# Layer 1 with DMA transposes, its scales taken through DRAM and its output matmuls one place later, a beginning written out by hand, and GpSimd additions placed behind their products in layer 2

## The chip, the core and the metric

The kernel runs on one core of one Trainium2 chip. The metric is device time in microseconds (us), as the median of a few runs. Beside it stands one profiled execution, whose trace gives the start, the length and the waits of the instructions on each engine: PE (TensorE), DVE (VectorE), ACT (ScalarE), POOL (GpSimd) and SP (SyncE, which here only issues DMAs).

## What is computed

Three sublayers, each followed by a residual addition and a layer norm, on x of shape (16, 256, 512), all float32:

```python
x = layernorm(x + attention(x))   # 16 heads of 32; causal softmax; q, k, v and output are "bitlinear":
                                  # weights rounded to -1, 0, 1 by their mean size,
                                  # each token rounded to 8 bits by its largest size
x = layernorm(x + mix(ctx, x))    # 32 heads of 8: kv_ij = ctx_i * ctx_j; long convolution of kv
                                  # along the sequence with a kernel for each head, plus D * kv;
                                  # out_j = sum over i of (that)_ij * x_i
x = layernorm(x + ffn(x))         # rms norm, gamma, 8-bit rounding, one ternary matmul 512 x 512
```

The norms and roundings use the sizes that the reference gives: epsilon 1e-5 in the layer norms, 127 steps for a token's largest value, and the mean absolute value for a weight.

## The kernel before

There are two stages. **Layer 1** (attention) takes one batch at a time, 256 tokens in NT = 2 tiles of 128. **Layer 2** (mixing and the feed-forward part) takes one head of the mixing at a time, 32 heads; the rows of a head are 8 inner places by 16 batches. The result of layer 1 stays in SBUF as `x1t`, already turned for layer 2.

Before layer 1 the five weights are loaded, summed (`part`), scaled (`w_mul`), rounded in two passes (L119 and L120 on DVE or POOL) and stored as bfloat16 (L121, on ACT).

Layer 1 is a pipeline over batches, written out by hand in `step(b)`: PE, ACT, DVE and POOL execute in the order of the calls. The scheduler orders SP's DMAs itself. Within a step four groups g of four heads each follow one another, and stages of other batches are set between their parts:

- `scan(b+1, g)`: scores for the maximum, in the PSUM tile `s` of four banks, of which there is one (L252 the mask, L259 the products); DVE takes the maximum (L264). `weigh(b, g)`: scores again in the same `s` (L292, L299), the exponential on ACT (L304, p), and two causal masks on POOL (L308). So `s` goes from scan to maximum to scores to exponential, and to the next scan.
- `values(b, g)`: p times v (L324), and the sums of p by a matmul with `col` (L331), whose right side is 256 and then 128 columns wide. `save_sums`, `divide_sums`, `divide`: the softmax's division, after a transpose on PE.
- `fetch_x`, `fetch_scales`, `fetch_scaled`, `fetch_rounded`: load of x, the tokens' scales, the scaled x on POOL (L135, xq_t), and its rounding on ACT (L141, xq_i). `turn_in`: the scales become a row along the free axis by a matmul with ones (L202), and the rounded x is turned by eight PE transposes (L148) with copies on ACT. `project_qk` and `project_v` (L220, L232) use it.
- `out_scales`, `out_scaled`, `out_rounded`, `turn_out`, `close`: the same for the attention's output (oq_t on DVE, oq_i on ACT, eight PE transposes), and the output matmuls (L387) with the residual on DVE. `moments`, `normalize`, `keep`: the layer norm and the transposed copy into `x1t`.

The rounded tiles of input and output come from one pool of SBUF and share one tag:

```python
def rounded(pool, tag, t):
    xi = pool.tile([P, E], BF16, name=f"{tag}_i", tag="q_i")   # pool ap, bufs=2
    nc.scalar.activation(xi, t, AF.Copy, bias=-MAGIC)
    return xi
```

Layer 2 is ordered by hand in the same way. For a head h, `block(h, lb)` makes the products of the quarter lb: 2(lb+1) matmuls (L546) into y, of which there are two, and on DVE `own` (L553, L556) and `turn` (L563); POOL adds turn to own (L567) directly behind. `read(h, lb)` sums six tiles into `tok` by PE transposes (L574): five of own, and q itself. `second_moments` and `second_norm` (DVE and ACT) end in fq_t (L135) and its rounding fq_i (L141); `turn(h)` transposes that on PE (L148), `feed_forward(h)` multiplies it (L641) and `finish(h)` writes the head out. POOL makes the next head's kv in `multiply` (L521); ACT copies its q.

Of the kernel before, what the change touches and what calls it, by code (L numbers as in the profile page):

```python
# [15 lines left out]
P = 128  # L16
# [16 lines left out]
def decoder_kernel(ctx: ExitStack, tc: tile.TileContext, x, ctx_t, w_q, w_k, w_v, w_o, ker, d_skip, gamma, w_f, out):  # L33
# [5 lines left out]
    first = const.tile([P, S // P, E], F32, name="first")  # L39
# [4 lines left out]
    wl_scope = ExitStack()  # L44
    wl = wl_scope.enter_context(tc.tile_pool(name="wload", bufs=1))
    wp = wl_scope.enter_context(tc.tile_pool(name="wpsum", bufs=1, space=PSUM))


    nc.sync.dma_start(first, x[0].rearrange("(t p) e -> p t e", p=P))
    raw = [wl.tile([P, NB, E], F32, name=f"raw{i}") for i in range(5)]  # L50
    for i, w in enumerate((w_q, w_k, w_v, w_o, w_f)):
        (nc.scalar, nc.sync)[i % 2].dma_start(raw[i], w.rearrange("(c p) o -> p c o", p=P))
    rows = wl.tile([XH, E + P], F32, name="rows")
    nc.scalar.dma_start(rows, ker)
    dsk = wl.tile([XH, 1], F32, name="dsk")
# [12 lines left out]
    mask_f = wl.tile([P, 2, P], F32, name="mask_f")  # L68
# [7 lines left out]
    nc.vector.tensor_copy(mask, mask_f)  # L76


    pick_f = wl.tile([P, NB], F32, name="pick_f")
# [8 lines left out]
    nc.vector.tensor_copy(pick, view(pick_f, 0, [[1, NB], [0, P]]))  # L88
# [10 lines left out]
    for i in range(5):  # L99
        t = raw[i].rearrange("p c o -> p (c o)")  # L100
        early = i < 3
        part = wl.tile([P, 1], F32, name=f"part{i}")
        if early:
            nc.vector.tensor_reduce(part, t, AX.X, ALU.add, apply_absolute_value=True)
        else:
            size = wl.tile([P, NB * E], BF16, name="size")
            nc.scalar.activation(size, t, AF.Abs, accum_out=part)
        total = wp.tile([P, 1], F32, name=f"total{i}", tag=f"total{i % 2}")
        nc.tensor.matmul(total, ones, part, start=True, stop=True)
        mean = wl.tile([P, 1], F32, name=f"mean{i}")  # L110
        nc.vector.tensor_scalar(mean, total, 1.0 / (E * E), 1e-5, ALU.mult, ALU.max if i < 4 else ALU.add)
        w_mul = wl.tile([P, 1], F32, name=f"w_mul{i}")
        nc.vector.reciprocal(w_mul, mean)
        nc.vector.reciprocal(w_inv[:, i : i + 1], w_mul)
        if i == 0:
            nc.vector.tensor_scalar(q_scale, w_inv[:, 0:1], 1.0 / math.sqrt(DH), None, ALU.mult)

        engine = nc.vector if i in (0, 2) else nc.gpsimd
        engine.tensor_scalar(t, t, w_mul, MAGIC, ALU.mult, ALU.add)  # L119
        engine.tensor_scalar(t, t, MAGIC + 1.0, MAGIC - 1.0, ALU.min, ALU.max)  # L120
        nc.scalar.activation(weights[i].rearrange("p c o -> p (c o)"), t, AF.Copy, bias=-MAGIC)  # L121
    wq, wk, wv, wo, wf = weights

    nc.vector.tensor_tensor(rows[:, P - 1 : P], rows[:, P - 1 : P], dsk, ALU.add)
    nc.sync.dma_start(taps, rows)
    wl_scope.close()


    kept = ctx.enter_context(tc.tile_pool(name="kept", bufs=1))
    x1t = kept.tile([P, XH, NB, XD, B], F32, name="x1t")  # L130
# [29 lines left out]
    with ExitStack() as l1:  # L160
        xp = l1.enter_context(tc.tile_pool(name="xp", bufs=2))
        ap = l1.enter_context(tc.tile_pool(name="ap", bufs=2))
        sp = l1.enter_context(tc.tile_pool(name="sp", bufs=3))
        hp = l1.enter_context(tc.tile_pool(name="hp", bufs=3))
        qk = l1.enter_context(tc.tile_pool(name="qk", bufs=3))
# [11 lines left out]
        def fetch_x(m, b):  # L177
            if b == 0:
                m.x = first
            else:  # L180
                m.x = xp.tile([P, NT, E], F32, name="xt")
                nc.sync.dma_start(m.x, x[b].rearrange("(t p) e -> p t e", p=P))

        def fetch_scales(m):
            amax = sp.tile([P, NT], F32, name="amax")
            nc.vector.tensor_reduce(amax, m.x, AX.X, ALU.max, apply_absolute_value=True)
            m.mul, m.inv = absmax_scales(sp, "x", amax, NT)
            m.v_mul = sp.tile([P, NT], F32, name="v_mul")
            nc.vector.tensor_scalar(m.v_mul, m.inv, w_inv[:, 2:3], None, ALU.mult)

        def fetch_scaled(m):
            m.xt = [scaled(ap, f"xq{t}", m.x[:, t, :], m.mul[:, t : t + 1], nc.gpsimd) for t in range(NT)]
            m.diag = kp.tile([P, NT, P], F32, name="diag")
            for t in range(NT):
                nc.gpsimd.tensor_scalar(m.diag[:, t, :], ident, m.inv[:, t : t + 1], None, ALU.mult)
# [4 lines left out]
        def turn_in(m):  # L200
            row = ps.tile([P, S], F32, name="row", tag="misc")
            nc.tensor.matmul(row, ones, m.diag.rearrange("p t k -> p (t k)"), start=True, stop=True)  # L202
# [5 lines left out]
            m.p = {}  # L208
            m.qt = qk.tile([P, NB, S], F32, name="qt")
            m.kt = qk.tile([P, NB, S], F32, name="kt")  # L210
            m.va = qk.tile([P, NT, NH, DH], F32, name="va")

        def project_qk(m, i):
            dst, w, scale = ((m.qt, wq, q_scale), (m.kt, wk, w_inv[:, 1:2]))[i % 2]
# [14 lines left out]
        def project_v(m, t):  # L229
            acc = ps.tile([P, NH, DH], F32, name="acc_v", tag="misc")  # L230
# [55 lines left out]
        def weigh(m, g):  # L286
# [25 lines left out]
            m.p[g] = p  # L312

        def values(m, g):
# [13 lines left out]
            for j, (q0, src) in enumerate(((0, slice(0, S)), (P, slice(S, S + P)))):  # L328
                for r in range(4):
                    rows = slice(DH * r, DH * (r + 1))  # L330
                    nc.tensor.matmul(  # L331
                        m.sums[rows, q0:S], col[:, g, :], p[:, r, src],
                        start=(g == 0 and j == 0), stop=(g == NB - 1 and j == 1),
# [8 lines left out]
        def save_sums(m):  # L342
            m.st = kp.tile([P, S], F32, name="sums_s")
            nc.vector.tensor_copy(m.st, m.sums)

        def divide_sums(m):
# [6 lines left out]
            m.o = ap.tile([P, NT, E], F32, name="o")  # L353
# [17 lines left out]
        def out_scaled(m):  # L371
            m.ots = [scaled(ap, f"oq{t}", m.o[:, t, :], m.mul_o[:, t : t + 1]) for t in range(NT)]
# [4 lines left out]
        def turn_out(m):  # L377
            m.oit = kp.tile([P, NT, NB, P], BF16, name="oit")
            for t in range(NT):
                transposed(ps, m.oit[:, t], m.oi[t])  # L380

        def close(m):
# [8 lines left out]
            m.st6 = sp.tile([P, NT, 6], F32, name="st")  # L391
            nc.vector.bn_stats(m.st6[:, 0, :], m.r1[:, 0, :])

        def moments(m):
            mv = m.mv = sp.tile([P, NT, 2], F32, name="mv")
            nc.vector.bn_stats(m.st6[:, 1, :], m.r1[:, 1, :])
            for t in range(NT):
                nc.vector.bn_aggr(mv[:, t, :], m.st6[:, t, :])
# [15 lines left out]
        def keep(m, b):  # L414
            nh = P // XD
            for t in range(NT):
                tp = ps.tile([P, NB, P], F32, name="tp1", tag="misc")
                for c in range(NB):
                    nc.tensor.transpose(tp[:, c, :], m.r1[:, t, c * P : (c + 1) * P], ident)
                nc.scalar.copy(  # L420
                    x1t[:, t * nh : (t + 1) * nh, :, :, b].rearrange("p h c i -> p c h i"),
                    tp.rearrange("p c (h i) -> p c h i", i=XD),
                )
# [5 lines left out]
        def step(b):  # L429


            for g in range(NB):
                on(scan, b + 1, g)
                if g == 0:
                    on(fetch_x, b + 3, b + 3)
                    on(fetch_again, b - 1, b - 1)
                    on(turn_in, b + 2)
                    on(moments, b - 2)
                    on(values, b - 1, NB - 1)
                    on(weigh, b, 0)  # L440
                    on(save_sums, b - 1)
                    on(project_qk, b + 2, 0)
                    on(normalize, b - 2)
                    on(divide_sums, b - 1)
                    on(divide, b - 1, 0)
                    on(divide, b - 1, 1)
                elif g == 1:
                    on(project_qk, b + 2, 1)
                    on(out_scales, b - 1)
                    on(values, b, 0)  # L450
                    on(weigh, b, 1)
                    on(project_qk, b + 2, 2)
                    on(keep, b - 2, b - 2)
                elif g == 2:
                    on(out_scaled, b - 1)
                    on(project_v, b + 2, 0)
                    on(values, b, 1)
                    on(weigh, b, 2)
                    on(project_qk, b + 2, 3)
                    on(fetch_scales, b + 3)  # L460
                    on(project_v, b + 2, 1)
                    on(out_rounded, b - 1)
                else:
                    on(turn_out, b - 1)
                    on(lay, b + 1, b + 1)
                    on(fetch_scaled, b + 3)
                    on(values, b, 2)
                    on(weigh, b, 3)
                    on(close, b - 1)
                    on(lay_turned, b + 1, b + 1)  # L470
                    on(fetch_rounded, b + 3)

        by_hand = {mybir.EngineType.PE, mybir.EngineType.Activation, mybir.EngineType.DVE, mybir.EngineType.Pool}
        on(fetch_x, 0, 0)
        on(fetch_scales, 0)
        on(fetch_scaled, 0)
# [266 lines left out]
```

## Time and profile before

| what | value |
|---|---|
| time, median of 3 runs | 1001.84 us (1001.75 to 1002.99) |
| profiled execution | 1000.92 us; span 999.2 us, clock 0.977 |
| PE busy | 886.3 us (89%) |
| DVE busy | 731.0 us (73%) |
| POOL busy | 493.9 us (49%) |
| ACT busy | 415.7 us (42%) |
| first scan of layer 1 starts | 45.8 us |
| step 0 / step 1 / step 13 of layer 1 start (copy `low`) | 61.9 / 87.7 / 416.6 us |
| first product of layer 2 starts | 514.3 us |

Shares are of the span. A busy share is an average over stages with different limits, so it is read by stage. "Idle before, releaser" beside an instruction says how long its engine had stood still and what it waited for last. The last columns of a stretch are the TensorE clock that was granted (1.00 is full), the busy share of the DMA engines, and GB/s. The page's list of DMA issues gives KB for each and the median time from issue to landing.

### The profile page before, as it was taken

What the parts mean: (1) busy time and instruction counts of PE and PEld (TensorE: products, weight loads), DVE (VectorE), ACT (ScalarE), POOL (GpSimd) and SP (SyncE); (2) the same over time, 40 slices, a digit from 0 to 9 for tenths busy, and PEclk for the clock granted to TensorE, in tenths of its full rate; (3) what the DMA queues carried; (4) which work ended last, traced back from release to release, by engine and by line L of the source; (5) the groups of instructions that cost most, each with busy time, mean ns of one, the idle gap of its engine ahead of it and who ended that gap; (6) DMA issues with size and microseconds to landing.
All of it is one profiled execution on the core that took longest, in us unless ns stands there. A gap on an engine that the chain in (4) does not pass through costs nothing.

```text
span 999.2 us, 21479 instructions
## 1 busy us (share of the span) xinstructions
PE 886.3 (89%) x8554; PEld 639.6 (64%) x8554; DVE 731.0 (73%) x1819; ACT 415.7 (42%) x651; POOL 493.9 (49%) x569
## 2 busy tenths in 40 slices
PE   1489999999999999997669999999999999999993
PEld 1356666666666666665437777777777777777772
DVE  6465777777777777766326888888888888888885
ACT  2533566666656656655531322222232223223222
POOL 4412322323223323312238777777777777677761
PEclk9999999999999999999959999999999999999996
DMA  9000111010111110000032122212212221222100
GB/s 318 25 23 23 44 44 44 26 41 23 44 44 44 44 44 23 23 23 23 12 95 53 49 74 64 70 53 74 64 53 70 65 73 49 74 64 63 44 22 22
DMA packets 54739, 53.19 MB, mean 53 GB/s; under 512 B 19120, under 2 KB 35504, under 8 KB 54640
## 3 DMA queue, kind: packets, MB, share of 16 engines
q1 hardware_dynamic: 52816, 48.33, 15.7%
q10 hardware_dynamic: 1824, 3.49, 1.0%
q8 instruction: 68, 1.11, 0.5%
q14 instruction: 31, 0.25, 0.1%
HBM read 43.34 MB, written 8.47 MB: 52 GB/s over the span
## 4 chain that ended last, share of the span: by engine, by line
PE 57%; DVE 28%; ACT 6%; issue 4%; DMA 2%; POOL 2%; SPq 0%; ACTq 0%; DVEq 0%; POOLq 0%
PE y L546 11%; PE acc L220 6%; PE s L292 6%; PE pv L324 5%; PE tok L574 5%; PE s L259 4%; DVE own L553 4%; PE sums L331 4%; DVE turn L563 3%; PE acc_f L641 3%; PE acc_o L387 3%; PE acc_v L232 3%; PE tp L148 3%; DVE full L601 2%; PE s L252 2%
## 5 line engine op out<-in xcount | busy, mean ns | idle before, releaser
L546 PE MATMUL y<-kv,w 128*128 128x288 f32 x1280 | 335.5, 410 | 4.4 <-DMA c<-in_ctx_t 2.9
L546 PEld LDWEIGHTS y<-kv,w 128*128 128x128 f32 x1280 | 235.3, 192 | 60.9 <-POOL kv L521 6.1
L567 POOL TENSOR_TENSOR own<-own,turn 128x512 f32<-128x512 f32 x128 | 162.3, 1268 | 125.1 <-DVE inv_root L597 64.0
L308 POOL TENSOR_SCALAR_AFFINE_SELECT p<-p 128x512 f32<-128x512 f32 x128 | 78.5, 638 | 256.5 <-ACT p L304 256.5
L521 POOL TENSOR_TENSOR kv<-c 128x512 f32<-128x512 f32 (+1 forms) x192 | 186.3, 991 | 3.3 <-DMA w<-taps 3.3
L264 DVE TENSOR_REDUCE nmax<-s 128x4 f32<-128x512 f32 (+1 forms) x128 | 116.7, 954 | 42.3 <-PE s L259 41.1
L553 DVE TENSOR_TENSOR own<-y,q 128x512 f32<-128x512 f32 x128 | 88.2, 689 | 76.8 <-PE y L546 66.6
L304 ACT ACTIVATE p<-s 128x1536 f32<-128x1536 f32 x64 | 93.1, 1454 | 88.4 <-PE s L299 88.4
L574 PE MATMUL tok<-ident,own 128*128 128x128 f32 x640 | 90.7, 273 | 0.0
L590 ACT ACTIVATE root<-quarter 128x2 f32<-128x2 f32 x64 | 13.0, 203 | 163.4 <-DVE quarter L588 163.4
L574 PEld LDWEIGHTS tok<-ident,own 128*128 128x128 f32 x640 | 74.1, 141 | 8.9
L220 PE MATMUL acc<-xit,w 128*128 128x256 bf16 x512 | 67.8, 277 | 5.8 <-ACT xit L149 5.8
L563 DVE TENSOR_TENSOR turn<-y,q 128x384 f32<-128x384 f32 x128 | 70.0, 547 | 0.0
L292 PE MATMUL s<-qt,kt 32*128 32x256 f32 (+1 forms) x1024 | 60.6, 351 | 2.6 <-DVE nmax L264 2.5
L220 PEld LDWEIGHTS <-w 128*128 128x128 bf16 x512 | 46.1, 99 | 23.3 <-issue 13.4
L259 PE MATMUL s<-kt,qt 32*128 32x128 f32 (+1 forms) x1024 | 60.5, 351 | 0.0
L324 PE MATMUL pv<-p,va 128*32 128x256 f32 (+1 forms) x1024 | 55.6, 332 | 4.7 <-POOL p L308 3.3
L292 PEld LDWEIGHTS s<-qt,kt 32*128 32x128 f32 x1024 | 47.1, 186 | 17.1 <-issue 14.8
L649 ACT ACTIVATE res<-r,shift,res 128x512 f32<-128x512 f32 x32 | 26.0, 813 | 71.9 <-DVE shift L605 71.9
L331 PE MATMUL sums<-p,col 128*32 128x256 f32 (+1 forms) x1024 | 54.4, 329 | 0.0
L224 DVE SCALAR_TENSOR_TENSOR qt<-acc,q_scale,inv_row 128x512 f32<-128x512 f32 x32 | 24.0, 750 | 39.5 <-PE acc L220 39.4
L622 ACT ACTIVATE x<-tok,shift,res 128x512 f32<-128x512 f32 x32 | 24.9, 777 | 65.0 <-DVE shift L605 65.0
(126 smaller groups left out, 1391.1 us busy)
## 6 DMA issues: line engine op xcount, KB each, us to landing
xr<-in_x SPq DMA_DIRECT2D x16, 512.0 KB, 3.6
c<-in_ctx_t SPq DMA_DIRECT2D x32, 256.0 KB, 3.4
w<-taps SPq DMA_DIRECT2D x32, 256.0 KB, 4.1
out_y<-res SPq DMA_DIRECT2D x32, 256.0 KB, 2.0
xt<-in_x SPq DMA_DIRECT2D x15, 512.0 KB, 3.6
c<-in_ctx_t SPq DMA_DIRECT2D x32, 128.0 KB, 3.2
raw<-in_w_q ACTq DMA_DIRECT2D x1, 1024.0 KB, 8.8
raw<-in_w_k SPq DMA_DIRECT2D x1, 1024.0 KB, 11.5
```

The source lines that it names most:

```text
L220: nc.tensor.matmul(acc[:, j, :], w[:, c, o * P : (o + 1) * P], m.xit[:, c].rearrange("p t k -> p (t k)"), start=(c == 0), stop=(c == NB - 1),)
L259: nc.tensor.matmul(s[:, r, lo:hi], m.qt[rows, g, q0 : q0 + P], m.kt[rows, g, 0:nk], start=False, stop=True, skip_group_check=True,)
L264: nc.vector.tensor_reduce(view(m.nmax, t * NH + g, [[NB, 4]]), s[:, :, cols], AX.X, ALU.max, negate=True)
L292: nc.tensor.matmul(s[:, r, lo:hi], m.kt[rows, g, k0 : k0 + P], m.qt[rows, g, q0:S], start=(lo == 0), stop=False, skip_group_check=True,)
L324: nc.tensor.matmul(acc[rows, q0:S], m.va[:, j, 4 * g + r, :], p[:, r, src], start=(j == 0), stop=(j == 1), skip_group_check=True, tile_pos ...
L331: nc.tensor.matmul(m.sums[rows, q0:S], col[:, g, :], p[:, r, src], start=(g == 0 and j == 0), stop=(g == NB - 1 and j == 1), skip_group_ch ...
L521: nc.gpsimd.tensor_tensor(kv[:, :, at : at + n * B].rearrange("p c (i b) -> p c i b", b=B), c[:, :, i : i + n, :], c[:, :, i + d : i + d + ...
L546: nc.tensor.matmul(y[:, Y0 + k * HALF : Y0 + (k + 1) * HALF], lhs, kv[:, mb, k * HALF : (k + 1) * HALF], start=(mb == 0), stop=(mb == lb),)
L553: nc.vector.tensor_tensor(own[:, 0:4, :], view(y, Y0 + AT, [[P, 4], [1, P]]), view(q, base, [[B, 4], [1, P]]), ALU.mult)
L563: nc.vector.tensor_tensor(view(t, B, [[P + B, 3], [1, P]]), view(y, Y0 + AT + P, [[P, 3], [1, P]]), view(q, base, [[0, 3], [1, P]]), ALU.mult,
L567: nc.gpsimd.tensor_tensor(own[:, 0:4, :], own[:, 0:4, :], t, ALU.add)
L574: nc.tensor.matmul(tok[:, lb, :], lhsT=part, rhs=ident, is_transpose=True, start=(n == 0), stop=(n == len(parts) - 1),)
```

## The change

**Layer 1.** From batch 2 on, the rounded input and, for every batch, the rounded output are turned by DMA transposes on SP's queue (`turn_in` for batch b+3, `turn_out`), not by PE. The scales are written to DRAM as a line and read back to all partitions (`fetch_line`), where a matmul with ones had made the row. `both`, the sum on POOL of two parts of p, makes the second sums matmul complete, so that the first need only be 128 wide. The output's scaling moves from DVE to POOL, `save_sums` from DVE to ACT. `close` is called for b-2 instead of b-1, in the second group. The order of the whole step is new, and SP's DMAs follow the order of the calls too.

**The beginning.** The weights load into the space of `x1t` (`lent`), and their sums, scales and roundings are single calls placed by hand: w_q and w_k on DVE, w_v's rounding on POOL behind the first scans' inputs, w_o and w_f in steps -1 and 0 (`begin_late`).

**Layer 2.** q's own term is folded into own by (y + 1) x q on DVE, so `read` sums five tiles. `add` (POOL) is called apart from `block` and later. `turn(h-2)` comes after block 0 of the next step, where `turn(h-1)` stood after block 3; `feed_forward` and `finish` move with it.

```diff
-        by_hand = {mybir.EngineType.PE, mybir.EngineType.Activation, mybir.EngineType.DVE, mybir.EngineType.Pool}
+        by_hand = {mybir.EngineType.PE, mybir.EngineType.Activation, mybir.EngineType.DVE, mybir.EngineType.Pool, mybir.EngineType.SP}
...
+        def fetch_line(m):
+            line = lines_pool.tile([NT, P], F32, name="line")
+            nc.sync.dma_start(line.rearrange("t p -> p t"), m.inv)
+            m.inv_row = ap.tile([P, S], F32, name="inv_row")
+            nc.sync.dma_start(m.inv_row, bass.AP(line.tensor, line.offset, [[0, P], [1, S]]))
...
         def turn_in(m):
-            row = ps.tile([P, S], F32, name="row", tag="misc")
-            nc.tensor.matmul(row, ones, m.diag.rearrange("p t k -> p (t k)"), start=True, stop=True)
-            m.inv_row = ap.tile([P, S], F32, name="inv_row")
-            nc.scalar.copy(m.inv_row, row)
             m.xit = ap.tile([P, NB, NT, P], BF16, name="xit")
             for t in range(NT):
-                transposed(ps, m.xit[:, :, t, :], m.xi[t])
+                nc.sync.dma_start_transpose(m.xit[:, :, t, :], m.xi[t])
...
+            both = bp.tile([P, 4, P], F32, name="both")
+            nc.gpsimd.tensor_tensor(both, p[:, :, P : 2 * P], p[:, :, 2 * P : 3 * P], ALU.add)
+            m.p[g], m.both[g] = p, both
...
-            for j, (q0, src) in enumerate(((0, slice(0, S)), (P, slice(S, S + P)))):
+            for q0, src in ((0, p[:, :, 0:P]), (P, m.both[g])):
                 for r in range(4):
                     nc.tensor.matmul(
-                        m.sums[rows, q0:S], col[:, g, :], p[:, r, src],
+                        m.sums[rows, q0 : q0 + P], col[:, g, :], src[:, r, :],
...
-            m.ots = [scaled(ap, f"oq{t}", m.o[:, t, :], m.mul_o[:, t : t + 1]) for t in range(NT)]
+            m.ots = [scaled(ap, f"oq{t}", m.o[:, t, :], m.mul_o[:, t : t + 1], nc.gpsimd) for t in range(NT)]
...
-                transposed(ps, m.oit[:, t], m.oi[t])
+                nc.sync.dma_start_transpose(m.oit[:, t], m.oi[t])
...
+            # the new order of step(b)
+            scan(b+1, 0); fetch_x(b+4); fetch_again(b-1); project_qk(b+2, 0)
+            values(b-1, 3); save_sums(b-1); weigh(b, 0); divide_sums(b-1); divide(b-1, 0 and 1)
+            scan(b+1, 1); project_qk(b+2, 1); values(b, 0); out_scales(b-1); weigh(b, 1)
+            fetch_scaled(b+3); out_scaled(b-1); fetch_rounded(b+3); turn_in(b+3); close(b-2)
+            begin_late(b+4, 0)      # b < 1: sum, scale and first rounding of w_o, w_f
+            scan(b+1, 2); moments(b-2); out_rounded(b-1); turn_out(b-1); project_qk(b+2, 2)
+            values(b, 1); weigh(b, 2); project_qk(b+2, 3); project_v(b+2, 0); normalize(b-2)
+            scan(b+1, 3); project_v(b+2, 1); values(b, 2); weigh(b, 3); keep(b-2, 0 and 1)
+            lay(b+1); lay_turned(b+1); fetch_scales(b+4); fetch_line(b+4); values_scale(b+4)
...
+            nc.vector.scalar_tensor_tensor(
+                own[:, 0, :], view(y, Y0 + AT, [[1, P]]), 1.0, view(q, base, [[1, P]]), ALU.add, ALU.mult
+            )
             nc.vector.tensor_tensor(
-                own[:, 0:4, :], view(y, Y0 + AT, [[P, 4], [1, P]]), view(q, base, [[B, 4], [1, P]]), ALU.mult
+                own[:, 1:4, :], view(y, Y0 + AT + P, [[P, 3], [1, P]]), view(q, base + B, [[B, 3], [1, P]]), ALU.mult
             )
...
-            nc.gpsimd.tensor_tensor(own[:, 0:4, :], own[:, 0:4, :], t, ALU.add)
-            terms.insert(0, view(q, base, [[1, P]]))
...
+                on(multiply, h + 1, 0); on(add, h - 1, 3)
                 on(block, h, 0)
-                on(feed_forward, h - 2)
+                on(turn, h - 2)
                 on(read, h - 1, 2)
-                on(multiply, h + 1, 0)
+                on(multiply, h + 1, 1)
                 on(block, h, 1)
-                on(finish, h - 2, h - 2)
+                on(feed_forward, h - 2); on(add, h, 0)
                 on(read, h - 1, 3)
-                on(multiply, h + 1, 1)
+                on(multiply, h + 1, 2)
                 on(second_moments, h - 1)
                 on(block, h, 2)
                 on(copy, h + 1)
+                on(add, h, 1)
                 on(read, h, 0)
-                on(multiply, h + 1, 2)
+                on(finish, h - 2, h - 2)
                 on(multiply, h + 1, 3)
                 on(second_norm, h - 1)
                 on(block, h, 3)
-                on(turn, h - 1)
+                on(add, h, 2)
                 on(read, h, 1)
```

The step's new order is shown condensed, several calls to a line. The beginning by hand, in the order of its calls: scales, rounding and PE transposes of batch 0; size of w_q (DVE) and w_k (ACT); scale, rounding and store of each; scales of batch 1; size of w_v (ACT); rounding of batch 1; q and k of batch 0; PE transposes of batch 1; scale, rounding (POOL) and store of w_v.

## The prediction

> **What bounds the kernel now.** I read the page's 40 slices first (two stages, a slow seam at slices 19 to 21), then busy time by stretch, then the timeline of one period of each stage. In the first view the columns are start, length, busy time of PE, weight loads, DVE, ACT and POOL (instructions in brackets), then the granted clock.
>
> ```profile
> 180.00:300.00 120.00, 118.05 (x1723) 80.72 (x1720) 87.87 (x172) 73.97 (x103) 33.89 (x54) 1.00 0.11 37
> ...
> 486.00:487.00 1.00, 1.00 (x20) 0.50 (x12) 0.00 (x0) 0.37 (x1) 0.00 (x0) 0.50 0.00 0
> ...
> 700.00:850.00 150.00, 140.13 (x745) 108.29 (x744) 124.56 (x370) 42.29 (x83) 112.44 (x105) 1.00 0.21 62
> ```
>
> Layer 1 is TensorE end to end (118 of 120 us). Layer 2 has PE at 93% and DVE at 83%. The timeline (start, length, engine) gives the periods and two limits behind PE:
>
> ```profile
> 252.28 0.37 ACT L284 COPY low<-tpn 128x256 bf16<-128x256 bf16 x1 [0.41 <-PE tpn L282]
> 279.67 0.37 ACT L284 COPY low<-tpn 128x256 bf16<-128x256 bf16 x1 [0.41 <-PE tpn L282]
> ...
> 450.01 0.60 PE L252 MATMUL s<-mask,ident_h 128*128 128x256 bf16 x4 [0.16 <-ACT p L304]
> 453.51 0.94 PE L292 MATMUL s<-qt,kt 32*128 32x256 f32 x16 [0.60 <-DVE nmax L264]
> 454.71 1.45 ACT L304 ACTIVATE p<-s 128x1536 f32<-128x1536 f32 x1 [2.01 <-PE s L299]
> 456.22 0.60 PE L252 MATMUL s<-mask,ident_h 128*128 128x256 bf16 x4 [0.58 <-ACT p L304]
> ...
> 484.28 0.92 PE L148 MATMUL tp<-ident_h,oq_i 128*128 128x128 bf16 x8 [2.13 <-ACT oq_i L141]
> 487.30 1.67 PE L292 MATMUL s<-qt,kt 32*128 32x256 f32 x16
> ...
> 716.05 0.61 DVE L135 TENSOR_SCALAR fq_t<-xn,mul 128x512 f32<-128x512 f32 x1
> 717.43 0.40 PE L148 MATMUL tp<-ident_h,fq_i 128*128 128x128 bf16 x4 [0.89 <-ACT fq_i L141]
> 720.71 1.76 PEld L546 LDWEIGHTS y<-kv,w 128*128 128x128 f32 x8
> 723.03 0.69 DVE L553 TENSOR_TENSOR own<-y,q 128x512 f32<-128x512 f32 x1 [0.32 <-PE tok L574]
> ```
>
> One step (a batch) takes 27.39. Late in layer 1, where PE has little left, a group of heads still takes 6.21 (450.01 to 456.22): one s buffer goes scan, maximum, scores, exponential, next scan. Four groups make 24.8, so layer 1 can gain at most about 2.6 a step. The clock halved after a PE gap of 2.13, and L292 took 1.67 instead of 0.94. In layer 2 a head takes 14.49, of which PE waits 0.89 for fq_i.
>
> **The change part by part.**
>
> *PE in layer 1.* Removed per step, start to start: row 0.53 (253.48 to 254.01), input transposes 0.72, output transposes 0.85, and sums over 256 instead of 384 columns, 0.64 x 1/3 = 0.21, four times: 2.95. PE would need 24.4. It is no longer the bound.
>
> *The chain that takes over.* In a normal group: scan 1.40, projection 0.97, values 1.20, to the scores 3.57; the scores' weight load to the exponential 1.20; exponential and next scan 1.51: 6.28. Three groups keep that. The second does not. POOL now runs, in order, the masks of the second group, the sum `both`, fetch_scaled, out_scaled; ACT runs exponential 1, xq_i twice, oq_i twice, ot, exponential 2. xq_i and oq_i share a tag with two buffers, so oq_i may be written only when the DMA transposes have read xq_i. ACT therefore waits for a DMA, and ot and exponential 2 are queued behind it, PE's fourth scan behind those. Before, PE had read the same buffers at once. From exponential 1 to exponential 2: 1.45, gap 0.13, masks 1.23, `both` 1.25 (L567, the same POOL addition, 1.27 each), xq_t twice 1.37, hop 0.1, xq_i 0.61, L, oq_i 0.57, ot 0.3 = 7.0 + L. L runs from the end of the second xq_i to the landing of its transpose.
>
> No transpose by DMA is in this trace. From below: the 256 KB store of out_y lands in 2.0 us, L = 2.1. Nearest row: 128 KB of c in 256-byte pieces,
>
> ```profile
> out_y<-res SPq DMA_DIRECT2D x32, 256.0 KB, 2.0
> c<-in_ctx_t SPq DMA_DIRECT2D x32, 128.0 KB, 3.2
> ```
>
> L = 3.3. Against the change speaks the Trainium skill, VectorE: DVE Perf Modes, "The three transpose paths": 1309 ns for 128x128 by DMA. Four blocks are an estimated 5.2, a second transpose queued behind the first brings L to about 10. I take 4.0, nearer the row: that 128 KB take 3.2 where 256 KB in longer pieces take 3.4 says pieces count and not bytes, and a transpose writes more, shorter pieces.
>
> *The clock.* PE's idle before the fourth scan is about L. Gaps of 2.13 (at 484) and 3.02 (at 61.6) were each followed by about 3.2 us at 0.50; one of 1.60 (at 462) was not. TensorE: Matmul & The Clock Gate, Part 1, puts the fall after an idle window of about 3.4 us. By the page only L above 3.4 costs; by the row, which decides, any L above about 2. 3.2 us at half speed delay the last group's scores by 1.6. A step is 3 x 6.28 + 7.0 + 4.0 + 1.6 = 31.44.
>
> Input and output meet from step 1 to step 12. Before, those took 328.9 (87.69 to 416.60); now 12 x 31.44 = 377.3: **+48.4**. Step 13 has no input: 18.84 + 6.4 = 25.3 for 27.4, **-2.1**. Step 14 +0.3. In step 15 sums waits for `both`, a group 5.5 instead of 5.05: +0.6.
>
> *Costed at nothing in layer 1.* save_sums on ACT (0.42) lies before an exponential that comes later. The line to DRAM and back (two DMAs of 2 to 4 us, behind one another on SP) has a step and a half before a projection reads it. The output's transposes have until the next step's close, about 18 us. SP now runs in program order: four transposes, two line DMAs and two loads at 0.4 to 0.6 issue each fill under 5 of 31 us. If a transpose held SP for more than 5 us, SP would be next. SP waits for the line's landing before it may read it back; the next x is queued behind that, and has more than a step. PE halves nothing else: its other gaps, half a microsecond a group, stay under the 1.60. At the end of layer 1 close waits for a DMA instead of PE and ACT (+2.9: POOL 1.4, ACT 0.6, L, instead of 2.5), but c is then loaded before the last close, while POOL's first kv (511.60) waited 3.25 for DMA: 0 together.
>
> *The beginning.* Scales of x0 (8.4), POOL and 8 transposes (13.3), copies (14.4), the sum over w_k on ACT (1.91 + 0.19, 16.6). w_q: sum ends 11.9, scale 14.4, two roundings at the uncontended 1.26 and 1.21 (L119, L120 at 24.76 and 26.13), store 1.91: 18.8. w_k the same from 17.7: 22.1. Projections to 24.3, first scan 26.5, for 45.8 before. Then: w_v's two roundings on POOL (1.98 + 1.89, 31.3), store (33.2), xq_i (34.4), sum over w_o (36.5), and w_o's total stands on PE ahead of the third scan. Two scans, two projections, four v halves and lay follow: step 0 starts at 48.1 for 61.7, -13.6. In step 0 the sum over w_f stands in ACT ahead of exponential 2 and its total on PE ahead of a scan: 1.45 + 0.13 + 1.23 + 1.25 + 1.37 + 0.1 + 0.61 + 2.1 + 0.4 + 4.77 = 13.4, and 3 x 6.28: 32.2 for 25.75. Left: **-7.1**.
>
> *Layer 2.* PE loses four q transposes a head (0.11 each) and the place where it waits for fq_i moves from behind block 3 to behind block 0 of the next head. DVE pays: own is split, 128x384 at 0.47 (L563) and scalar_tensor_tensor of 128x128 at 0.26 (L556's 0.20 start to start, plus the 0.06 that L617 costs over L553), for 0.60: +0.13 four times, DVE's busy path 12.53 to 13.05. Let s be the end of fq_t. fq_i and its transpose follow at s + 0.78 (716.65 to 717.43), 0.23 for it, 0.45 for read, block 1 loads at s + 1.46, its products at + 2.32 (720.71 to 723.03): s + 3.78. DVE in between has two groups, 2.8, and idles 1.0. After it: group 1.40, r3 1.87, second_moments 1.73, group 1.40, finish 0.83, second_norm 3.02: s + 14.03. So 14.03 a head for 14.49, 31 times: **-14.3**. POOL's additions (10.6 of busy in 14) come free in time: the latest, of block 3, ends at about s + 4.4 for a read at s + 4.2, with 1.5 to spare on DVE. c is asked for only behind out_y and lands about when its first product is due; the cover is that same 1.5. At the end of the program the last head's transpose, product and finish follow one another as before: 0.
>
> Sum: +48.4 - 1.2 - 7.1 - 14.3 = +25.8 on the profiled 1000.92 (span 999.2), which is 0.9 under the median 1001.84: about **1027.6**.
>
> **The rivals.**
> Faster (26 in 100): L is short. The price is L a step, in 12 steps, plus 1.6 where the gap cools PE. The rest gives 22.6; 12 x (25.84 + L - 27.41) eats it at L = 3.45 with a warm clock, at 1.85 with a cold one. At 2.1 and warm: 12 x 0.53 = 6, total -16, 986. For it: out_y's 2.0, and Advanced Engine Details and Errata, "X-Bar Transpose (TRN2)", calls transposes as fast as regular DMAs. Against it: the 3.2 of small pieces.
> Much slower (12): the pair takes 10: 12 x 6 more, 1100.
> Layer 2 gives nothing (10): DVE's 0.52 a head with no wait removed, because fq_i still ends last. 14.5 a head, 1042. For it: PE's wait moves, it does not vanish.
> The change not doing what it says in layer 1 is the likeliest case itself: the place that output matmuls move hides their own transposes but not the buffer.
>
> **How the numbers follow.** Likeliest 52 in 100, with L from 3 to 6: 1013 to 1052. Faster 26, much slower 12, no gain in layer 2 10. Leaving out the far ends of the first and third: 987 to 1078. About 0.2% (2 us) is what a measurement of this kernel can tell: faster 0.27, same 0.03, slower 0.70.
>
> **What would show it.** Right: ACT oq_i waiting for a DMA transpose once a step, 3 to 5 us; PE's longest wait before the fourth scan, then clock below 1; steps of about 31; PE busy under 85% in layer 1; heads of 14.0 with DVE over 90%. Wrong: steps under 28 (L or the cold clock), a first scan far from 26, step 0 far from 48, heads at 13.3 (fq_i no bound) or above 14.5.

## The result and the profile after

The changed kernel takes 1033.51 us (median of 4 runs, 1030.16 to 1036.1), the kernel before 1001.8 beside it: a ratio of 1.031 (1.028 to 1.035). It is slower, and 6 us above the predicted 1027.6. Its profiled execution took 1032.65, with a span of 1030.8 and a granted clock of 0.943.

The same stretches of both stages as before (start, length, busy time of PE, weight loads, DVE, ACT, POOL, clock):

```profile
180.00:300.00 120.00, 99.81 (x1458) 67.32 (x1465) 76.47 (x148) 56.41 (x78) 51.34 (x66) 0.95 0.26 58
700.00:850.00 150.00, 143.25 (x735) 110.10 (x745) 131.84 (x440) 44.33 (x88) 114.28 (x110) 1.00 0.23 68
```

In layer 1 PE fell from 118 to 100 of 120 us: it is not the bound any more, and its clock is below 1. In layer 2 PE is at 95% and DVE at 88%. One normal step of layer 1, ACT's instructions in the timeline with what ended each wait:

```profile
247.46 0.43 ACT L323 COPY low<-tpn 128x256 bf16<-128x256 bf16 x1
...
256.99 1.45 ACT L343 ACTIVATE p<-s 128x1536 f32<-128x1536 f32 x1 [1.15 <-PE s L338]
261.79 1.30 ACT L162 ACTIVATE xq_i<-xq_t 128x512 bf16<-128x512 f32 x2 [3.35 <-POOL xq_t L156]
266.35 0.63 ACT L162 ACTIVATE oq_i<-oq_t 128x512 bf16<-128x512 f32 x1 [3.26 <-DMA xit<-xq_i]
267.15 0.63 ACT L162 ACTIVATE oq_i<-oq_t 128x512 bf16<-128x512 f32 x1 [0.18 <-DMA xit<-xq_i]
267.69 0.35 ACT L378 COPY ot<-pv 128x256 f32<-128x256 f32 x1
267.94 1.45 ACT L343 ACTIVATE p<-s 128x1536 f32<-128x1536 f32 x1
...
275.17 1.45 ACT L343 ACTIVATE p<-s 128x1536 f32<-128x1536 f32 x1 [1.07 <-PE s L338]
...
278.22 0.43 ACT L323 COPY low<-tpn 128x256 bf16<-128x256 bf16 x1
```

The step takes 30.76 where it took 27.39. The two xq_i end at 263.09, the DMA has read the first of them at 266.35 and the second at 267.15, and only then may ACT write oq_i, the copy of ot and the exponential behind it. On PE the wait shows ahead of the first v projection, and the clock falls behind it (the granted clock is 0.50 from 268 to 271; 0.60 and 0.94 are the full-speed lengths of the last two):

```profile
268.09 0.58 PE L271 MATMUL acc_v<-w,xit 128*128 128x512 bf16 x1 [3.87 <-ACT ot L378]
268.90 1.06 PE L271 MATMUL acc_v<-w,xit 128*128 128x512 bf16 x2 [0.22 <-issue]
269.75 1.06 PE L291 MATMUL s<-mask,ident_h 128*128 128x256 bf16 x4
270.74 1.16 PE L298 MATMUL s<-kt,qt 32*128 32x128 f32 x16
```

Not every step is like this one. From the end of the second xq_i to the start of the second oq_i it is 4.06 here, and 3.15 to 4.76 in steps 1 to 12 (median 3.5). Step 2 takes 39.2, steps 7, 8 and 9 take 32.7, 31.7 and 34.0. In step 9, as in 2 and 8, ACT and DVE stand although PE has finished what they use:

```profile
340.47 0.37 SPq L213 DMA_DIRECT2D line<-x_v  x1
...
345.45 0.34 PE L338 MATMUL s<-low,pick 32*128 32x256 bf16 x8
345.72 0.44 PE L391 MATMUL tps<-ident,sums_s 128*128 128x128 f32 x2
346.00 1.04 PE L400 MATMUL ops<-ident,ot 128*128 128x128 f32 x8
348.25 1.45 ACT L343 ACTIVATE p<-s 128x1536 f32<-128x1536 f32 x1 [3.04 <-PE ops L400]
348.29 0.37 DVE L394 RECIPROCAL rec<-tps 128x16 f32<-128x16 f32 x2 [3.18 <-PE ops L400]
348.72 0.34 SPq L215 DMA_DIRECT2D inv_row<-line  x1
```

The scores are done at 345.8, and the exponential, which normally follows after about 0.1, starts at 348.25. DVE's reciprocal goes at the same moment, and shortly after it SP, whose turn comes when the write of `line` has landed, 8 us after its issue. Neither ACT nor DVE is itself held: both wait for PE's semaphore, and the trace records its increment for the scores, whose matmuls end at 345.79, only at 348.22. The median delay from the end of PE's work to this record is 0.01 us.

A head of layer 2, from one fq_t to the next, takes 13.69 where it took 14.49:

```profile
707.44 0.49 DVE L156 TENSOR_SCALAR fq_t<-xn,mul 128x512 f32<-128x512 f32 x1
708.70 0.40 PE L169 MATMUL tp<-ident_h,fq_i 128*128 128x128 bf16 x4 [0.54 <-ACT fq_i L162]
...
711.70 0.29 DVE L664 SCALAR_TENSOR_TENSOR own<-y,q 128x128 f32<-128x128 f32 x1 [1.13 <-PE y L656]
...
721.13 0.48 DVE L156 TENSOR_SCALAR fq_t<-xn,mul 128x512 f32<-128x512 f32 x1
```

Put together by the copies `low`, which start the steps, and the first product of layer 2 (y, 514.33 before, 570.67 after):

| part | before | after | difference | predicted |
|---|---|---|---|---|
| start of step 0 | 61.9 | 50.1 | -11.8 | -13.6 |
| step 0 | 25.8 | 36.0 | +10.3 | +6.5 |
| steps 1 to 12 | 328.9 | 380.1 | +51.2 | +48.4 |
| steps 13 and 14 | 52.4 | 51.0 | -1.4 | -1.8 |
| step 15 to the first product | 45.3 | 53.5 | +8.1 | +0.6 |
| first product to the end | 484.9 | 460.1 | -24.7 | -14.3 |
| sum (spans) | 999.2 | 1030.8 | +31.6 | +25.8 |

The sum came closer than its parts: three of them are off by 4 to 10 us, and they partly cancel.

### The profile page after: what moved, and what is told of

Same layout as the page of the kernel before. It is cut to its first block, busy times and chain, and to the rows that moved or that the text cites. A ratio compares the mean times of both kernels' runs of the same rounds, so it can differ in the third digit from the quotient of the medians.

```text
span 1030.8 us, 20858 instructions
## 1 busy us (share of the span) xinstructions
PE 860.5 (83%) x8097; PEld 612.1 (59%) x8158; DVE 706.8 (69%) x1897; ACT 387.9 (38%) x597; POOL 570.3 (55%) x637
## 4 chain that ended last, share of the span: by engine, by line
DVE 29%; PE 26%; issue 18%; POOL 9%; DMA 6%; ACT 5%; SPq 0%; POOLq 0%; ACTq 0%; DVEq 0%
PE y L656 8%; DVE st L692 4%; POOL p L347 3%; POOL both L353 3%; DVE turn L677 3%; PE s L298 3%; PE acc_f L751 3%; DVE full L711 2%; DVE r L753 2%; DMA xit<-xq_i 2%; ACT p L343 2%; PE tok L685 2%; ACT fq_i L162 2%; DVE amax L734 2%; PE s L331 2%
## 5 line engine op out<-in xcount | busy, mean ns | idle before, releaser
L631 POOL TENSOR_TENSOR kv<-c 128x512 f32<-128x512 f32 (+1 forms) x192 | 182.1, 965 | 100.5 <-DMA c<-in_ctx_t 73.7
L353 POOL TENSOR_TENSOR both<-p 128x512 f32<-128x512 f32 x64 | 81.2, 1268 | 5.3
L664 DVE SCALAR_TENSOR_TENSOR own<-y,q 128x128 f32<-128x128 f32 x128 | 36.3, 284 | 56.5 <-PE y L656 54.9
L257 PE MATMUL acc<-xit,w 128*128 128x256 bf16 x512 | 71.4, 288 | 2.1 <-ACT w L146 2.1
L271 PE MATMUL acc_v<-w,xit 128*128 128x512 bf16 x113 | 39.4, 455 | 39.6 <-ACT ot L378 37.9
L667 DVE TENSOR_TENSOR own<-y,q 128x384 f32<-128x384 f32 x128 | 69.9, 546 | 0.0
L291 PE MATMUL s<-mask,ident_h 128*128 128x256 bf16 x256 | 44.2, 301 | 30.0 <-ACT p L343 28.7
L298 PE MATMUL s<-kt,qt 32*128 32x128 f32 (+1 forms) x1024 | 68.1, 386 | 0.0
L366 PE MATMUL pv<-p,va 128*32 128x256 f32 (+1 forms) x1024 | 59.0, 349 | 7.3 <-POOL p L347 5.8
```

Of the source, the lines that this page charges most:

```text
L257: nc.tensor.matmul(acc[:, j, :], w[:, c, o * P : (o + 1) * P], m.xit[:, c].rearrange("p t k -> p (t k)"), start=(c == 0), stop=(c == NB - 1),)
L298: nc.tensor.matmul(s[:, r, lo:hi], m.qt[rows, g, q0 : q0 + P], m.kt[rows, g, 0:nk], start=False, stop=True, skip_group_check=True,)
L353: nc.gpsimd.tensor_tensor(both, p[:, :, P : 2 * P], p[:, :, 2 * P : 3 * P], ALU.add)
L631: nc.gpsimd.tensor_tensor(kv[:, :, at : at + n * B].rearrange("p c (i b) -> p c i b", b=B), c[:, :, i : i + n, :], c[:, :, i + d : i + d + ...
```

## The experiments

**1. oq_i in buffers of its own.** One line of the changed kernel:

```diff
-        xi = pool.tile([P, E], BF16, name=f"{tag}_i", tag="q_i")
+        xi = pool.tile([P, E], BF16, name=f"{tag}_i", tag=f"{tag[0]}_i")
```

> The changed kernel with one edit: the rounded attention output oq_i gets buffers of its own, so that ACT may write it while the DMA transposes still read xq_i. Theory (the buffer wait sets the second group's length): exponential 1 to exponential 2 falls from 10.95 to about 7.8 us (1.45 + 0.13 + 1.23 + 1.26, four POOL scalings of 0.68, 0.6 for the last rounding, 0.4 for ot), PE's wait before the first v projection from 3.9 to about 0.7, the clock stays at 1.00, so that the group after it costs 6.3 and not 7.2. A normal step goes from 30.7 to 26.6, twelve steps give 49, the total is about 984 (978 to 992). Rival (the four scalings on POOL and PE's own chain set it, the wait for the transpose is only what happens to end last): exponential 2 moves by less than 1 us, total above 1020.

Measured: 990.09 (0.987 of the kernel before, 0.986 to 0.989). ACT in the same part of a step:

```profile
266.89 1.45 ACT L343 ACTIVATE p<-s 128x1536 f32<-128x1536 f32 x1 [1.15 <-PE s L338]
271.69 1.30 ACT L162 ACTIVATE xq_i<-xq_t 128x512 bf16<-128x512 f32 x2 [3.35 <-POOL xq_t L156]
273.14 1.30 ACT L162 ACTIVATE oq_i<-oq_t 128x512 bf16<-128x512 f32 x2 [0.15 <-POOL oq_t L156]
274.35 0.35 ACT L378 COPY ot<-pv 128x256 f32<-128x256 f32 x1
274.60 1.46 ACT L343 ACTIVATE p<-s 128x1536 f32<-128x1536 f32 x1
...
280.89 1.45 ACT L343 ACTIVATE p<-s 128x1536 f32<-128x1536 f32 x1 [1.13 <-PE s L338]
```

Exponential 1 to exponential 2 is 7.71 where it was 10.95, and the next one follows after 6.29 where it was 7.23: 3.24 for the wait and 0.94 for the cold clock. PE waits 0.63 ahead of the v projection. Normal steps take 26.63. The transposes are the same DMAs as before, so it is the shared buffer that cost, not the transpose. The irregular steps stayed (36.2 for step 2, 31.3 for step 9).

**2. The layer 2 alone.** The kernel before, with the changed code from `with ExitStack() as l2` on; its list of hand-ordered engines, without SP, is kept.

> The kernel before with the changed layer 2 alone (q's term added by VectorE as y + 1, the GpSimd additions behind the products, the turn of fq_i a place later); its beginning and layer 1 are untouched. Theory (the head went from 14.49 to 13.69, 31 times 0.80): 977 (975 to 979), heads of 13.7. Rival (the prediction's 14.3, the rest being the later and warmer start of layer 2 in the changed kernel): 986 to 988. Rival 2 (it depends on something of layer 1): over 995.

Measured: 981.61 (0.980, 0.978 to 0.981), 20.7 us less, between the theory and its rival. The head takes 13.83, not 13.69. The whole difference of 0.14 is fq_t: 0.62 here, 0.48 in the changed kernel, for the same instruction. Experiment 8 takes that up.

**3. The scales' row by a matmul, and both edits together.** The row is made as in the kernel before, without DRAM; the calls stand at the end of the first group:

```diff
+            on(scales_row, b + 3)   # POOL: diag = ident * inv, twice; PE: ones x diag; ACT: copy
             on(scan, b + 1, 1)
...
-            on(fetch_line, b + 4)
```

> The changed kernel, but the scales reach their row as in the kernel before (POOL's two diagonals, a matmul with ones, a copy on ACT, all placed at the end of the first group a step ahead), and not by DRAM; the DMA transposes stay. Theory (in steps 2, 8 and 9 every engine stood still until the scattered write of the 256 scales had landed, 8.0 us after its issue; that costs about 3.5 + 1.7 + 2.4 us and two cold clocks of 1.6): those steps come down to the 30.7 of the others, xr and xt land in under 5 us for 7, the rest stays, total 1018 to 1025. Rival (the stops come from something else, for instance the loading of instructions): stops of 2 to 4 us remain in some steps and the total is 1031 to 1036, with PE's 0.5 more a step hidden.

> The changed kernel with both edits: oq_i in buffers of its own, and the scales' row by a matmul. If the two costs are separate, the sum of both gains: 1033 - 49 - 12 = 972 (965 to 980), with even steps of about 26.6. If the slow write only mattered because the transposes queued behind it, less than the sum: about 983, as with the buffers alone. If neither is the cause, above 1015.

Measured: 1107.74 and 1058.95, outside both expectations, and both for a reason of the experiment. POOL and PE around the row in the first of them:

```profile
285.17 1.26 POOL L354 TENSOR_TENSOR both<-p 128x512 f32<-128x512 f32 x1
286.41 1.19 POOL L212 TENSOR_SCALAR diag<-ident,x_v 128x128 f32<-128x128 f32 x2
287.65 1.22 PE L214 MATMUL row<-diag,ones 128*128 128x256 f32 x2 [4.12 <-POOL diag L212]
```

POOL takes its instructions in order. The diagonals stood behind the masks and `both` of the group, which wait for the exponential, and PE stood 4.12 for them with the next scan queued behind. A normal step took 37.6. The pair still says two things. Own buffers for oq_i are worth 48.8 (1107.74 to 1058.95) here too. And in neither kernel do an exponential and a reciprocal stand together as in steps 2, 8 and 9 of the changed one.

**4. The same with POOL's diagonals a place earlier**, ahead of the first group's masks, once with oq_i's own buffers and once without:

```diff
+            if b >= 0:
+                on(scales_diag, b + 3)
             on(weigh, b, 0)
...
             on(divide, b - 1, 1)
+            on(scales_row, b + 3)
```

> As the run with oq_i in buffers of its own, and the scales' row by a matmul again, this time with POOL's two diagonals ahead of the first group's masks, where POOL is idle, so that the row does not wait for them. Theory (the matmul's price was POOL's order alone, and the stops of all engines in two steps, 9.6 and 4.6 us with the cold clock behind them, come from the scattered write of the scales): every step from 1 to 12 takes 26.6 to 26.9, no engine stands still in step 2, the total is 990 - 16 + 2 = 976 (972 to 980). Rival (the stops belong to the loading of instructions and come without the write too): 988 to 993, with stops of over 3 us left.

> The changed kernel with the scales' row by a matmul, POOL's diagonals ahead of the first group's masks, and oq_i in the buffers that it shares with xq_i, as in the change. Theory (the write of the scales cost the stops in steps 2, 8 and 9 and nothing else; the wait of ACT for the transposes stays): every step from 1 to 12 is 30.4 to 31.0, ACT waits 3 us for the transposes in each, total 1033 - 8.5 - 1.2 - 3.3 = 1020 (1016 to 1024). Rival (the write also slowed the transposes behind it): steps under 30 and a total under 1014.

Measured with own buffers: 972.54 (0.970, 0.969 to 0.972), with steps of 26.61 to 26.63 (step 10 takes 26.9, step 2 takes 28.3), and no such stop. Two POOL instructions moved ahead of three others, the two masks and `both`, took the time from 1058.95 to 972.54.

Measured without own buffers: 1023.65 (1019.09 to 1027.9), steps of 30.6 to 31.4 in the profiled execution (one 32.5, and step 12 at 28.9), ACT still waiting up to 3.5 for the transposes. So the way of 256 scales through DRAM costs 18 us beside own buffers and 10 without. Each of the two costs shows without the other, but they do not simply add: own buffers gain 43 beside the write and 51 without it.

The stops are shown to come with this write: four kernels that have it show them (the changed one and experiments 1, 5 and 7; ACT idle for 2.3 to 6.0 ahead of an exponential whose scores are done), the five changed kernels that have the row by a matmul do not. It is the write and not the reading back, which SP issues only when the stop is over (348.72 above). In those four kernels PE's semaphore is recorded up to 5.3 after the end of PE's work, in the other five never more than 0.06. In step 2 of the changed one four of its increments, for groups of matmuls that end about 0.4 apart, are recorded 0.05 to 0.06 apart, at 125.35 to 125.52: the signals were late, and not the work. What inside the chip holds them is not shown.

**5. The place of c**. In layer 2 the pools of fp and op are opened ahead of those of c and w; the rest as in experiment 1.

> As the run with oq_i in buffers of its own, and layer 2 opens the pools of c and w behind two others, so that c's first buffers lie over memory of layer 1 that is free earlier than r1. Theory (first c is asked for only behind the last transposes of r1, which costs the 3.5 us between the last copy into x1t and the first product, 5.3 to 7.5 where the kernel before has 1.8): c is issued 10 us or more earlier and the first product follows the last copy by about 2 us: 990 - 4 = 986 (984 to 988). Rival (the first product waits for POOL's kv, which is late anyway, or for the table load): 989 to 991.

Measured: 983.11 (977.47 to 985.84), 7 less than experiment 1, more than expected. SP issues the first c at 496.23, before the last batches are closed:

```profile
496.23 0.67 SPq L622 DMA_DIRECT2D c<-in_ctx_t  x1
...
503.38 1.28 PE L656 MATMUL y<-kv,w 128*128 128x288 f32 x2 [3.16 <-DMA w<-taps]
```

In experiment 1 that was at 523.08, and the first product at 529.63. Now POOL's kv and the first products lie beside the end of layer 1, and what starts layer 2 is the last copy of x1t (521.85) and ACT's q. That is about 7 of the 8.1 in the table's fifth row.

**6. q's term on TensorE again**: experiment 2 with own as one instruction of 512 columns and six transposes instead of five.

> As the run of the kernel before with the changed layer 2 alone, but q's term stays a transpose on TensorE and own stays one instruction of 512 columns: only the places of the GpSimd additions and of fq_i's turn are changed. Theory (the gain comes from the places: PE no longer stands behind fq_i with a block queued behind it; the split of own is about neutral, 0.05 a group on DVE against 0.11 on PE): heads of 13.7 to 13.9, total 978 to 983 like that run's 981.6. Rival (PE's four transposes fewer are the gain): heads of 14.2 to 14.4, total 993 to 999.

Measured: 992.02 (0.989, 0.988 to 0.991), about 10 above the theory, and with a head of 14.16 next to the rival's range. By the totals the places give about half of the 20 us and the split the other half. The trace says how: again the difference to 13.83, 0.33, is fq_t, which now takes 0.96. The rest of the head is 13.2 here, in experiment 2 and in the changed kernel, against 13.9 in the kernel before. So that part is the places' gain, and the split acts through the length of fq_t alone, by when POOL's next product starts.

**7. The sum over w_f later**: in step 0 it stands behind the exponentials, and its scale and roundings in step 1; the rest as in experiment 1.

> As the run with oq_i in buffers of its own, but the sum over w_f stands on ACT at the end of step 0, behind its exponentials, and w_f's scale and rounding follow in step 1. Theory (in step 0 the sum and the total that PE waits for held the third scan and let the clock fall, 15.0 from exponential 1 to exponential 2): step 0 falls from 36.5 to about 28.5, step 1 grows by less than 1, total 982 (979 to 985). Rival (step 0 is slow because of the clock and the late start alone): total 988 to 991.

Measured: 970.83 (0.968, 0.967 to 0.970), 19 less than experiment 1. Step 0 falls from 36.5 to 27.8, as expected. The other part was not expected: step 2 falls from 36.2 to 28.6, because the stop there is gone, while step 9 still has one (30.8). So the write alone does not make a stop; that the two must coincide in time is argued, not shown.

**8. GpSimd's addition ahead of its product**: experiment 2 with two calls exchanged.

```diff
-                on(multiply, h + 1, 0)
                 on(add, h - 1, 3)
+                on(multiply, h + 1, 0)
```

> As the run of the kernel before with the changed layer 2 alone (981.6), but on GpSimd the addition of the block before stands ahead of the first product of the next head, so that no product of GpSimd is running when VectorE starts fq_t. Theory (a running product holds fq_t: it ended 0.28 us after the product in three kernels, 730.87 to 731.15, 724.55 to 724.83, 712.79 to 713.07; undisturbed it takes 0.48 or less): fq_t takes 0.48 for 0.62, the head 13.69 for 13.83, the total falls by 31 x 0.14 = 4.3 to about 977.3. Rival (fq_t's length has to do with where its tiles lie): fq_t stays 0.62, total 980.5 to 983.

Measured: 978.37 (0.976, 0.974 to 0.977); fq_t takes 0.48 and the head 13.69, both as the theory says. POOL and fq_t in experiment 6, in experiment 2, in this one and in the changed kernel, two lines each:

```profile
711.75 1.04 POOL L521 TENSOR_TENSOR kv<-c 128x512 f32<-128x512 f32 x1 [1.37 <-PE y L546]
712.11 0.96 DVE L135 TENSOR_SCALAR fq_t<-xn,mul 128x512 f32<-128x512 f32 x1
```

```profile
723.51 1.04 POOL L521 TENSOR_TENSOR kv<-c 128x512 f32<-128x512 f32 x1 [1.02 <-PE y L546]
724.21 0.62 DVE L135 TENSOR_SCALAR fq_t<-xn,mul 128x512 f32<-128x512 f32 x1
```

```profile
640.05 0.48 DVE L135 TENSOR_SCALAR fq_t<-xn,mul 128x512 f32<-128x512 f32 x1
642.03 1.27 POOL L673 TENSOR_TENSOR own<-own,turn 128x512 f32<-128x512 f32 x1 [3.22 <-DVE turn L567]
```

```profile
707.44 0.49 DVE L156 TENSOR_SCALAR fq_t<-xn,mul 128x512 f32<-128x512 f32 x1
709.99 1.04 POOL L631 TENSOR_TENSOR kv<-c 128x512 f32<-128x512 f32 x1 [3.26 <-DMA c<-in_ctx_t]
```

In the first two fq_t ends 0.28 after the product that was running (712.79 and 724.55). In the other two POOL stands idle. The Trainium skill, SBUF — State Buffer, "SBUF: two separate sides", says that GpSimd and some VectorE instructions take a pair of ports by an exclusive lock, for a whole instruction, and that the other one blocks. The four pairs agree with that.

**9. All four repairs**: own buffers for oq_i, the row by a matmul with early diagonals, w_f later, c's place.

> All four repairs together: oq_i in buffers of its own, the scales' row by a matmul with POOL's diagonals in its idle time, the sum over w_f at the end of step 0, c's buffers over memory that is free earlier. If the costs are separate: 972.5 - 8.8 (step 0) - 7.1 (the seam) = 957 (953 to 961). If the sum over w_f and the seam only moved the stops to other places (their runs still had the slow write): 965 to 970.

Measured: 959.72 (958.63 to 960.71), 0.957 of the kernel before (0.956 to 0.959), inside the range for separate costs and 3 short of the full sum. Step 0 takes 25.6, steps 3 to 12 take 26.61 to 26.64, and in layer 1 PE is back at 113 of 120 us:

```profile
180.00:300.00 120.00, 112.91 (x1702) 77.79 (x1707) 85.80 (x165) 66.59 (x93) 64.31 (x84) 1.00 0.24 63
```

This version beats both kernels: the change's parts were worth 4% once the waits that it had brought were gone.

## Why the prediction was right, and where it was not

- **The chain that takes over: right.** 7.0 + L from exponential 1 to 2 with L = 4.0 was to be 11.0; in the step shown 10.95 was measured, and L, from 263.09 to 267.15, is 4.06. In all of steps 1 to 12 it is 6.9 + L, with L from 3.15 to 4.76. Experiment 1 shows the cause. The choice of the c row (3.3) over the estimate for four blocks (5.2, from the Trainium skill, VectorE: DVE Perf Modes, "The three transpose paths") was the right one: a transpose of 128x512 lands 2.4 after its issue (median of the 58 landings recorded), which is less than half of that estimate. But the reason given for going from 3.3 up to 4.0 does not hold, so that part is luck: a transpose moved 512 packets of 256 bytes in the trace, just as many and as long as the 128 KB of c. L is longer than 2.4 because the second transpose stands behind the first on SP (issued at 263.73, landed at 267.07).
- **Where PE waits: wrong place, right price.** It waits ahead of the first v projection, whose release is the copy of ot, and not ahead of the fourth scan. The same copy was in the chain, so the sum is the same.
- **The cold clock: mis-sized both ways.** It was put at 1.6 a step and costs 0.94 in the step shown (7.23 to 6.29). A normal step is then 30.7 and not 31.44, 9 less in twelve steps. It is not the same in each: in steps 10 and 11 it costs 1.4 and 1.5, and in step 12, with a PE gap of 2.96 like the 2.97 to 2.99 of steps 8 to 11, the clock did not fall, and the step took 28.8. In step 0, where no cold clock was counted, it costs twice: exponential 0 to 1 takes 7.79 for 6.28, and the total to exponential 2 takes 7.8 for the 4.77 of the sum. This is enough for 36.0 instead of 32.2. The rule of the Trainium skill (TensorE: Matmul & The Clock Gate, Part 1: a fall after an idle window of about 3.4) would not have given the first of these: ahead of the scan at 56.23, which took 1.66 for 0.94, PE's gaps within 10 us were 1.86, 1.22 and 1.54. The measurement decides.
- **The line to DRAM, costed at nothing: wrong.** "Two DMAs of 2 to 4 us" was an assumption. Twelve of the 14 writes landed 7.7 to 8.4 after their issue, the other two 10.1 and 10.5, and the cover named (a step and a half) does hide this for the projection that reads the line. What had no cover is that PE's signals to other engines can be late while it is under way. In steps 1 to 12 the stops and the steps with late transposes made up for the 9 us of the point above, and a little more: +51.2 for +48.4 is right by two misses.
- **The seam: wrong.** "c is then loaded before the last close" failed. c's first buffers lay over r1, and SP waited 13.2 for the last transposes of r1. In the kernel before, other memory lay there. Nothing of the diff's layer 2 shows this; it is argued from the pool of x having moved out of layer 1's pools. That c's place was the cause is shown by experiment 5.
- **Layer 2: right in the mechanism, too small.** By the prediction's own path, from the end of fq_t (the start of the instruction behind it): the wait by PE 3.86 for 3.78, the groups 1.34 and 1.32 for 1.40 each, r3 1.79 for 1.87, second_norm with fq_t 2.82 for 3.02. The group was priced with 0.26 for the new instruction of 128x128, which takes 0.20 from start to start. Most of the rest is fq_t, 0.61 to 0.48, because POOL waits about 3 us for c, now issued behind out_y, and so is idle when fq_t runs. The prediction saw the late c and gave it no effect; it was a gain of about 31 x 0.14.
- **The beginning** came as worked out: the first scan's products at 26.89 for 26.5, w_o's total at 36.85 for 36.5; step 0 came 2 later, at 50.1 for 48.1.
- **The rivals.** A short L (faster) fell: 3.15 at the least, against the 1.85 that it needed with a cold clock. L of 10 fell too: 4.76 at the most. "Layer 2 gives nothing" fell: its part is 24.7 shorter, and 20.7 with layer 2 alone (experiment 2).

## What to carry to other kernels

Moving work from an engine to a DMA lengthens the time for which the source buffer is held; look for who writes that buffer next, and what is queued behind that instruction, before counting the saved work. Check what a DMA's landing and a pool's new place release, also where the change has no line. When the sum comes out right, compare it part by part: here three misses of 4 to 10 us partly cancelled.

## What the runs showed of the hardware

- A DMA of 256 values of 4 bytes from 128 partitions to DRAM landed 7.7 to 8.4 us after its issue in 12 of 14 cases and 10.1 and 10.5 us in two, while 512 KB of x landed in 3.6 in the kernel before. (The Trainium skill, DMA: Bandwidth & Descriptors, "Specifications", has pieces under 512 bytes written by read-modify-write; no run here shows what the 8 us consist of.) While it is under way, signals by which PE releases ACT and DVE can be recorded up to 5.3 us late, and ACT then stands idle for 2.3 to 6.0 us (both longest in experiment 1); without such a write they were never more than 0.06 late.
- Two DMA transposes of 128x512 bfloat16 occupy SP's queue for 2.5 to 3.4 us (the two pairs of step 6), and one mostly lands 2.4 us after its issue (median of 58; 4.0 at the most).
- One VectorE instruction, fq_t, took 0.48, 0.62 or 0.96 us depending on when a GpSimd product was running. In the changed kernel GpSimd, which came late, made VectorE faster.
- The granted clock fell to 0.50 for 3.4 us after PE gaps of 2.97 to 2.99 us in steps 8 to 11, and did not after one of 2.96 in step 12.
